# Start of a CIN kernel: transposes in another order, two weights read in memory order, and one block load moved to another queue

## The chip, the cores and the metric

One NeuronCore of one Trainium2 chip. The metric is the device time of one execution in microseconds (us), lower is better. Every execution, the timed ones too, comes with the span and the granted TensorE clock of its core. "Fast" runs are those within 1.5% of the fastest of their kernel; only those are compared. Ratios are the mean time of one kernel's fast runs over that of the kernel before in the same rounds, the first run of each left out, so they are not quite the ratios of the medians quoted beside them.

In the profile PE is TensorE (PEld its weight loads), DVE VectorE, ACT ScalarE, POOL GpSimd and SP SyncE. Where another engine needs the result of an instruction, the program has the instruction raise a semaphore, a counter that the other waits for. Where a wait ends and the profile finds no instruction that had just ended and raises that semaphore, it writes "another core or an unknown queue" in the chain and "remote" in the timeline. There is no other core in this program, so in the lines shown here these words mark semaphores that come late: in the kernel before, TensorE's semaphore records stand at 21.38 and 22.14 us, where the transposes that these waits are for stand as done at 15.64 and 15.87.

## The reference, cut to what matters

Three layers of a compressed interaction network on x (1024 x 39 x 64), then a dense layer to one number per sample:

```python
def _cin_layer(Xk, X0, W, b):          # W: (64, Hk * 39)
    Wr = W.reshape(64, Hk, 39)
    return einsum('bhe,bfe,ohf->boe', Xk, X0, Wr) + b[None, :, None]
for W, b in ((W0, b0), (W1, b1), (W2, b2)):
    Xk = _cin_layer(Xk, X0, W, b)
    outs.append(Xk.sum(axis=-1))
y = concatenate(outs, -1) @ fc_w.T + fc_b
```

Only a sum leaves the last layers, so the kernel folds W2 and fc_w into a small matrix v2, folds v2 and W1 into T, and puts W0 and T side by side as weights over pairs of fields. The main loop multiplies products of gathered rows of x by these weights.

## The kernel before

The parts that the change touches all lie ahead of the main loop; cuts are marked.

```python
# W2 with v: h is inside f, so a step of 39 floats in SBUF
w2v = w2s.rearrange("p (h f) -> p f h", f=F)
for k in range(2):
    for u in range(4):
        f0 = u // 2 * 19 + k * 10
        nc.tensor.matmul(pv[k][32*u : 32*u+32, 0:320], fc2[...], w2v[:, f0 : f0 + 10, :], ...)
# ...
halves = [slice(0, SUB), slice(SUB, BLK)]
for k, cols in enumerate(halves):
    for i in range(3):
        gather_rows(rt[0][:, i, cols], xh[k], i)          # GpSimd, indirect DMA
for k, cols in enumerate(halves):
    gather_rows(rt[0][:, 3, cols], xh[k], 3)
    nc.sync.dma_start(xd[0][0:F, cols], xh[k][0:F])
load(1)                                                   # second block, SP's queue
# ... W1 with v2 into pt, pv; copied to `part` and `rest`; then
for q in range(2):
    for k in (1, 0):                                      # upper rows, lower rows, upper, lower
        rows = slice(H * k, H * k + FT)
        turn_fields(pw[k], part, rows, (q + 1) * NA // 2, q * NA // 2)
turn_fields(pt[0], rest, slice(0, FT), NR)
for k in (1, 0):
    untwine(copies[k], 1, NA * k, NA, NA // 2, pw[k], FT)  # the copies of T into `both`
untwine(copies[1], 1, 2 * NA, NR, 1, pt[0], FT)
spin(3)                                                   # filler matmuls, read by nobody
```

`copies` is VectorE (DVE) for k = 0 and ScalarE (ACT) for k = 1. The pair weights, and so the first main matmul, need all copies of T.

Of the kernel before, what the change touches and what calls it, by code (L numbers as in the profile page):

```python
# [60 lines left out]
B, F, E, H = 1024, 39, 64, 64  # L61
FH = F * H
# [15 lines left out]
NA = 16  # L78
NR = F - 2 * NA
# [19 lines left out]
def cin_kernel(ctx: ExitStack, tc: tile.TileContext, x, w0t, b0, w1, b1, w2, b2, fc_w, fc_b, out):  # L99
    nc = tc.nc  # L100
# [13 lines left out]
    def bank(name):  # L114
        return psum.tile([128, MM], F32, name=name, tag="po")

    def load(n, engine=nc.sync):
        first = n % 2 * FT
        engine.dma_start(  # L119
            xd[n // 2 % NTAB][first : first + F].rearrange("f (b e) -> f b e", e=E),  # L120
            xv[:, n * BB : (n + 1) * BB, :],
        )

    def gather_rows(dst, table, k):
        nc.gpsimd.indirect_dma_start(  # L125
            dst, None, table, bass.IndirectOffsetOnAxis(ap=lists[:, k : k + 1], axis=0)
        )
# [12 lines left out]
    v2 = const.tile([128, H], F32, name="v2")  # L140
# [28 lines left out]
    with prep as prep:  # L169
        w2s = prep.tile([128, FH // 2], F32, name="w2s")  # L170
        w1s = prep.tile([128, FH // 2], F32, name="w1s")
        w0s = prep.tile([128, NW * H], F32, name="w0s")
        part = prep.tile([128, NA, H], F32, name="part")
# [41 lines left out]
        pv = [bank("pv") for _ in range(2)]  # L215
        pt = [bank("pt") for _ in range(2)]
# [5 lines left out]
        def spin(n=1, cols=MM // 2):  # L222
            for _ in range(n):
                nc.tensor.matmul(  # L224
                    idle[:, 0:cols],
                    nc.const_aps.tensor(1.0, (128, 128), F32),
                    nc.const_aps.tensor(1.0, (128, cols), F32),
                    start=True,
                    stop=True,
                )  # L230
# [10 lines left out]
        def new():  # L241
            used[0] += 1
            return tmp[:, used[0] - 1 : used[0]]

        def step(x, at, by, out=None):

            out = new() if out is None else out
            nc.vector.tensor_scalar(out, x, at, by, ALU.is_ge, ALU.mult)
            return out
# [4 lines left out]
        row, f0, j, extra, t, half, q = new(), new(), new(), new(), new(), new(), new()  # L254
# [2 lines left out]
        nc.vector.tensor_copy(row, place)  # L257
        nc.vector.tensor_scalar(parity[:, 1:2], place, 1, None, ALU.bitwise_and)
        nc.vector.tensor_scalar(third, third, 9, None, ALU.logical_shift_right)
        step(row, K, 1.0, extra)  # L260
        nc.vector.tensor_copy(f0, third)
        nc.vector.tensor_scalar(wide[:, 3], shifts[:, 2], row, None, ALU.add)
# [39 lines left out]
        nc.vector.tensor_tensor(field[4], q, step(q, F, -float(F)), ALU.add)  # L302
        nc.vector.tensor_tensor(field[4], field[4], step(q, 56, 11.0), ALU.add)


        nc.vector.memset(w1s[0:H, 0:1], 0.0)
        nc.sync.dma_start(w1s[0:H], w1[:, 0 : FH // 2])

        halves = [slice(0, SUB), slice(SUB, BLK)]
        for k, cols in enumerate(halves):  # L310
            for i in range(3):
                gather_rows(rt[0][:, i, cols], xh[k], i)
        for k, cols in enumerate(halves):
            gather_rows(rt[0][:, 3, cols], xh[k], 3)
            nc.sync.dma_start(xd[0][0:F, cols], xh[k][0:F])
        load(1)



        blocks = prep.tile([128, 2, 320], F32, name="blocks")  # L320
        w2v = w2s.rearrange("p (h f) -> p f h", f=F)
        for k in range(2):
            for u in range(4):
                f0 = u // 2 * 19 + k * 10
                nc.tensor.matmul(
                    pv[k][32 * u : 32 * u + 32, 0:320],
                    fc2[:, u % 2 * 32 : u % 2 * 32 + 32],
                    w2v[:, f0 : f0 + 10, :],
                    start=True,
                    stop=True,  # L330
                )
# [11 lines left out]
                    unit[H * s : H * s + F, H * s : H * s + F],  # L343
                )
        for k in range(2):
            nc.vector.transpose(blocks[:, k], pv[k][:, 0:320])
        column = blocks.rearrange("h k (f j) -> h (k f) j", j=32)[:, :, 0]
        for s, at in enumerate((2, 5)):
            rows = slice(H * s, H * s + H)
            nc.scalar.copy(v2[rows, F:FT], small[rows, at : at + 1])  # L350
        for s in range(2):
            rows = slice(H * s, H * s + H)
# [36 lines left out]
        for s, (a, n) in enumerate(((0, NW), (NW, F - NW))):  # L389
            untwine(copies[s], 0, a, n, 1, pw[s], F)  # L390
        spin()
        w1v = w1s.rearrange("o (h f) -> o f h", f=F)
        for s in range(2):
            rows = slice(H * s, H * s + H)
            nc.tensor.matmul(  # L395
                pv[s][rows, 0 : 32 * NR], v2[rows], w1v[rows, 2 * NA : F, :], start=True, stop=True
            )
        for s in range(2):
            rows = slice(H * s, H * s + H)
            for k in range(2):  # L400
                nc.tensor.matmul(  # L401
                    pt[s][H * k : H * k + H],
                    v2[rows],
                    w1v[rows, NA * k : NA * (k + 1), :].rearrange("o (t j) h -> o j t h", t=2),
                    start=True,
                    stop=True,
                )
        for s, copy in enumerate(copies):
            at = slice(32 * s, 32 * s + 32)
            copy(  # L410
                rest[:, :, at],
                pv[s][H * s : H * s + H, 0 : 32 * NR].rearrange("b (a h) -> b a h", h=32),
            )
        for q in range(2):
            for s, copy in enumerate(copies):
                fields = slice(q * NA // 2, (q + 1) * NA // 2)
                copy(
                    part[:, fields, 32 * s : 32 * s + 32],
                    pt[s].rearrange("b (a h) -> b a h", h=32)[:, fields],
                )  # L420

        def turn_fields(to, src, rows, n, start=0):
            for a in range(start, n, 2):
                m = min(2, n - a)
                nc.tensor.transpose(  # L425
                    to[0 : m * H, a // 2 * FT : a // 2 * FT + FT],
                    src[rows, a : a + m, :].rearrange("b a h -> b (a h)"),
                    unit[rows, rows],
                )

        spin()
        for q in range(2):
            for k in (1, 0):
                rows = slice(H * k, H * k + FT)
                turn_fields(pw[k], part, rows, (q + 1) * NA // 2, q * NA // 2)
        turn_fields(pt[0], rest, slice(0, FT), NR)
# [135 lines left out]
    p = {}  # L572
# [113 lines left out]
```

## Time and profile before

| | before |
|---|---|
| time, median of 4 | 755.05 us |
| main matmuls, busy and idle before them | 723.2 us, 0.0 us |
| first main matmul starts | 24.75 us |
| products of W1 (T) | 11.36 to 14.35 us |
| transposes of T | 14.91 to 15.87 us |
| copies of T begin | 17.86, 21.41, 22.16 us |

TensorE is full from the first main matmul to the last (0.0 us of idle time before the main matmuls), so the only room is the lead, the 25 us ahead of it. Read it as a chain: what the first main matmul waits for, and what that waits for. The lines of it stand in the prediction.

One trap of this profile: the granted clock is shown as 1.00 until the trace's first clock record, which lies at 4.2 us in this trace and between 4.0 and 20.6 us in the others. Whether TensorE was at full or at half clock (1.00 or 0.50 granted) before that is seen only from durations of equal work, such as the four filler records near 4.4 us. In the kernel before (timeline: start, duration, engine, line, operation):

```profile
4.33 0.92 PE L224 MATMUL idle<-const-float32-1.0 128*128 128x256 f32 x4
```

### The profile page before, as it was taken

The numbers are of one execution on the slowest core, as the hardware profiler recorded it, in microseconds if no ns is written. First come the engines' busy times: TensorE is split into PE (matmuls) and PEld (weight loads), VectorE is DVE, ScalarE is ACT, GpSimd is POOL, SyncE is SP. The second block draws the span as 40 slices with busy tenths as digits, with TensorE's granted clock in tenths as the row PEclk, the third lists the DMA queues.
The fourth block names the chain that finished last, engine by engine and source line by source line (L and its number), as shares of the span: only waits on it lengthen the run. The fifth ranks groups of instructions, "written<-read, shape, count | busy, mean of one in ns | idle before, by whom it ended". The sixth has DMA issues, their size and how long they took to land.

```text
span 753.2 us, 5294 instructions
## 1 busy us (share of the span) xinstructions
PE 741.6 (98%) x1913; PEld 324.5 (43%) x1913; DVE 643.1 (85%) x510; ACT 164.1 (22%) x225; POOL 320.5 (43%) x198
## 2 busy tenths in 40 slices
PE   7799999999999999999999999999999999999998
PEld 4344444444444444444444444444444444444443
DVE  4879998888998888889888898888889888898885
ACT  2122122222112212122222212222112221212222
POOL 6568632536333363442536333263532436343100
PEclk9899999999999999999999999999999999999999
DMA  8689977765758766566865758767576854737400
GB/s 213 226 305 367 369 311 252 292 254 174 288 181 328 257 230 269 169 271 245 309 246 192 288 167 317 258 237 261 176 286 224 332 225 162 287 137 307 167 1 0
DMA packets 60223, 180.40 MB, mean 240 GB/s; under 512 B 38415, under 2 KB 38480, under 8 KB 40229
## 3 DMA queue, kind: packets, MB, share of 16 engines
q0 software_dynamic: 24352, 169.12, 59.1%
q1 hardware_dynamic: 34235, 9.27, 5.4%
q10 hardware_dynamic: 1610, 1.67, 1.0%
q8 instruction: 15, 0.25, 0.1%
q14 instruction: 11, 0.09, 0.0%
HBM read 179.98 MB, written 10.60 MB: 253 GB/s over the span
## 4 chain that ended last, share of the span: by engine, by line
PE 97%; DMA 1%; DVE 1%; another core or an unknown queue 0%; POOL 0%; ACT 0%; issue 0%; DVEq 0%; ACTq 0%
PE po L504 96%; DMA w1s<-in_w 1%; PE idle L224 0%; PE pt L401 0%; POOL xh L210 0%; PE tr L488 0%; ACT both L382 0%; PE pv L395 0%; DVE g L543 0%; DVE pairs L453 0%; DVE sums L545 0%; ACT zq L542 0%; PE pw L425 0%; PE small L291 0%
## 5 line engine op out<-in xcount | busy, mean ns | idle before, releaser
L504 PE MATMUL po<-p,wa 128*128 128x512 f32 (+1 forms) x1792 | 723.2, 595 | 0.0
L163 DVE TENSOR_TENSOR p<-r 128x2048 f32<-128x2048 f32 (+2 forms) x196 | 434.8, 2247 | 86.1 <-PE po L504 81.7
L504 PEld LDWEIGHTS po<-p,wa 128*128 128x128 f32 (+1 forms) x1792 | 314.0, 190 | 405.5 <-issue 385.1
L125 POOL DMA_INDIRECT r<-xd,lists x124 | 246.8, 1991 | 355.5 <-DVE p L163 329.5
L523 ACT ACTIVATE z<-po,fc0s 64x512 f32<-64x512 f32 x124 | 84.6, 683 | 354.8 <-PE po L504 348.0
L517 ACT COPY g<-u 39x1024 f32<-39x1024 f32 x64 | 66.6, 1043 | 184.0 <-DVE sums L534 182.4
L529 DVE SCALAR_TENSOR_TENSOR g<-po,b0s,z 64x512 f32<-64x512 f32 x124 | 86.4, 734 | 0.0
L534 DVE TENSOR_REDUCE sums<-g 103x16 f32<-103x1024 f32 x62 | 75.6, 1220 | 2.2
L125 POOL DMA_INDIRECT u<-xd,lists x16 | 36.4, 2277 | 12.5 <-DMA xd<-in_x 8.0
L165 DVE TENSOR_TENSOR p<-u,v 128x2048 f32<-128x2048 f32 x16 | 36.6, 2285 | 0.3 <-PE tr L488 0.3
L125 POOL DMA_INDIRECT v<-xd,lists x16 | 18.0, 1127 | 4.9 <-issue 4.9
L125 POOL DMA_INDIRECT r<-xh,lists x8 | 7.7, 959 | 6.4 <-DVE fields_of L359 4.2
L224 PE MATMUL idle<-const-float32-1.0 128*128 128x256 f32 (+1 forms) x22 | 7.9, 487 | 0.8 <-PEq L673 0.8
L488 PE MATMUL tr<-unit,pairs 128*128 128x128 f32 x7 | 2.2, 318 | 6.3 <-DVE pairs L453 6.3
L382 DVE COPY both<-pw 64x390 f32<-64x390 f32 (+1 forms) x4 | 2.1, 523 | 6.4 <-remote 6.4
L543 DVE SCALAR_TENSOR_TENSOR g<-po,b0s,zq 64x512 f32<-64x512 f32 x4 | 3.0, 742 | 5.3 <-ACT zq L542 5.3
L489 ACT COPY wa<-tr 128x128 f32<-128x128 f32 x7 | 1.9, 266 | 19.9 <-PE tr L488 19.9
L224 PEld LDWEIGHTS idle<-const-float32-1.0 128*128 128x128 f32 x22 | 4.8, 241 | 3.2 <-issue 2.6
L453 DVE TENSOR_TENSOR pairs<-both 128x6 f32<-128x6 f32 (+27 forms) x50 | 5.4, 175 | 0.4 <-ACT both L382 0.4
L542 ACT ACTIVATE zq<-po,fc0s 64x512 f32<-64x512 f32 x4 | 2.7, 684 | 10.2 <-PE po L504 10.2
L488 PEld LDWEIGHTS tr<-unit,pairs 128*128 128x128 f32 x7 | 1.1, 160 | 8.4 <-ACT pairs L457 6.7
L119 POOL DMA_DIRECT2D xd<-in_x x4 | 4.1, 1062 | 0.0
(93 smaller groups left out, 46.4 us busy)
## 6 DMA issues: line engine op xcount, KB each, us to landing
xd<-in_x SPq DMA_DIRECT2D x27, 312.0 KB
r<-xd,lists POOLq DMA_INDIRECT x124
xd<-in_x POOLq DMA_DIRECT2D x4, 312.0 KB
w2s<-in_w ACTq DMA_DIRECT2D x1, 624.0 KB
xh<-in_x ACTq DMA_DIRECT2D x2, 156.0 KB
w1s<-in_w ACTq DMA_DIRECT2D x1, 312.0 KB
w1s<-in_w SPq DMA_DIRECT2D x1, 312.0 KB
xd<-xh SPq DMA_DIRECT2D x2, 156.0 KB
```

What stands on the lines that cost most here:

```text
L119: engine.dma_start(xd[n // 2 % NTAB][first : first + F].rearrange("f (b e) -> f b e", e=E), xv[:, n * BB : (n + 1) * BB, :],)
L125: nc.gpsimd.indirect_dma_start(dst, None, table, bass.IndirectOffsetOnAxis(ap=lists[:, k : k + 1], axis=0))
L163: nc.vector.tensor_tensor(p[:, cols], r[:, i, cols], r[:, k, cols], ALU.mult)
L165: nc.vector.tensor_tensor(p, ut[n // 2 % 2], vt[n // 2 % 2], ALU.mult)
L224: nc.tensor.matmul(idle[:, 0:cols], nc.const_aps.tensor(1.0, (128, 128), F32), nc.const_aps.tensor(1.0, (128, cols), F32), start=True, sto ...
L453: nc.vector.tensor_tensor(out, diagonal(a, b, sa, sb), diagonal(b, a, sb, sa), ALU.add)
L488: nc.tensor.transpose(tr[:, at], pairs[:, c], unit)
L504: nc.tensor.matmul(po[n + h][m], wa[w, c, :], p[w, bass.ts(m, MM)], start=c == opens[n + h], stop=c == closes[n + h],)
L517: nc.scalar.copy(gt[H : H + F], ut[n // 2 % 2][h : h + F, bass.ts(m, SUB)])
L523: nc.scalar.activation(z[m // 2][:, bass.ts(m % 2, MM)], po[n][m][H:128], AF.Identity, bias=fc0s[H:128])
L529: nc.vector.scalar_tensor_tensor(gt[0:H, at], po[n][m][0:H], b0s, z[m // 2][:, at], ALU.add, ALU.mult)
L534: nc.vector.tensor_reduce(sums[:, b_at : b_at + SB], gt.rearrange("p (b e) -> p b e", e=E), AX.X, ALU.add)
```

## The change

Five parts, of two intents: shorten the chain (W1 loaded earlier; W1 and W2 read as they lie in memory, with the reordering left to copies that are made anyway; the transposes that ScalarE waits for issued first), and take the second block's load off SP.

```diff
+        nc.vector.memset(w1s[0:H, 0:1], 0.0)            # was after the field lists
+        nc.sync.dma_start(w1s[0:H], w1[:, 0 : FH // 2])
         ...
             for i in range(3):
                 gather_rows(rt[0][:, i, cols], xh[k], i)
+            if not k:
+                load(1, nc.gpsimd)
         ...
-        load(1)
-        w2v = w2s.rearrange("p (h f) -> p f h", f=F)
+        w2v = w2s.rearrange("p (h f) -> p h f", f=F)
-                    w2v[:, f0 : f0 + 10, :],
+                    w2v[:, :, f0 : f0 + 10],
         ...  (the DVE transposes read PSUM with the step instead)
-        w1v = w1s.rearrange("o (h f) -> o f h", f=F)
+        w1v = w1s.rearrange("o (h f) -> o h f", f=F)
         ...  (the copies to part and rest read PSUM with the step instead)
-        for q in range(2):
-            for k in (1, 0):
+        for k in (1, 0):
+            for q in range(2):
```

More of the change, by code (lines that the diff above doesn't have):

```diff
@@ L303, in cin_kernel @@
         nc.vector.tensor_tensor(field[4], field[4], step(q, 56, 11.0), ALU.add)
-        nc.vector.memset(w1s[0:H, 0:1], 0.0)
-        nc.sync.dma_start(w1s[0:H], w1[:, 0 : FH // 2])
         halves = [slice(0, SUB), slice(SUB, BLK)]
@@ L345, in cin_kernel @@
         for k in range(2):
-            nc.vector.transpose(blocks[:, k], pv[k][:, 0:320])
+            nc.vector.transpose(
+                blocks[:, k].rearrange("p (f h) -> p f h", h=32),
+                pv[k][:, 0:320].rearrange("p (h f) -> p f h", f=10),
+            )
         column = blocks.rearrange("h k (f j) -> h (k f) j", j=32)[:, :, 0]
@@ L395, in cin_kernel @@
             nc.tensor.matmul(
-                pv[s][rows, 0 : 32 * NR], v2[rows], w1v[rows, 2 * NA : F, :], start=True, stop=True
+                pv[s][rows, 0 : 32 * NR], v2[rows], w1v[rows, :, 2 * NA : F], start=True, stop=True
             )
@@ L403, in cin_kernel @@
                     v2[rows],
-                    w1v[rows, NA * k : NA * (k + 1), :].rearrange("o (t j) h -> o j t h", t=2),
+                    w1v[rows, :, NA * k : NA * (k + 1)],
                     start=True,
@@ L411, in cin_kernel @@
                 rest[:, :, at],
-                pv[s][H * s : H * s + H, 0 : 32 * NR].rearrange("b (a h) -> b a h", h=32),
+                pv[s][H * s : H * s + H, 0 : 32 * NR].rearrange("b (h a) -> b a h", h=32),
             )
+        slots = part.rearrange("b (j t) h -> b t j h", t=2)
         for q in range(2):
             for s, copy in enumerate(copies):
-                fields = slice(q * NA // 2, (q + 1) * NA // 2)
-                copy(
-                    part[:, fields, 32 * s : 32 * s + 32],
-                    pt[s].rearrange("b (a h) -> b a h", h=32)[:, fields],
-                )
+                fields = slice(q * NA // 4, (q + 1) * NA // 4)
+                src = pt[s].rearrange("b (h t j) -> b t j h", t=2, h=32)
+                copy(slots[:, :, fields, 32 * s : 32 * s + 32], src[:, :, fields])
         def turn_fields(to, src, rows, n, start=0):
```

## The prediction

> **What bounds the kernel now.** I read the page first (busy times, the chain of waits by line), then the pieces of that chain in order of time, then the timeline and the waits of the first 30 us, then busy time by stage. The page says where the time is:
>
> ```profile
> PE 97%; DMA 1%; DVE 1%; another core or an unknown queue 0%; POOL 0%; ACT 0%; issue 0%; DVEq 0%; ACTq 0%
> ...
> L504 PE MATMUL po<-p,wa 128*128 128x512 f32 (+1 forms) x1792 | 723.2, 595 | 0.0
> ```
>
> The main matmuls occupy 723.2 of 753.2 us with 0.0 us of idle time before them. In the chain they run from 24.96 us to 748.27 us; only small transposes and last-layer products of the same engine stand between. After them come 2.8 us of tail (an activation, a multiply, a sum, the last product). The change touches neither loop nor tail. What it can move is the first 24.96 us, plus the speed of the first few matmuls. That lead is one dependent chain; its pieces:
>
> ```profile
> 5.75 5.47 DMA w1s<-in_w
> 11.22 0.14 issue
> 11.36 0.70 PE pv L395 x2
> 12.05 0.29 PE pt L401
> 12.34 0.12 PE pv L395
> 12.46 1.89 PE pt L401 x5
> 14.35 0.63 PE idle L224 x2
> 14.98 0.66 PE pw L425 x16
> 15.64 0.22 PE pt L425 x4
> 15.87 1.98 PE idle L224 x6
> ...
> 18.30 0.42 ACT both L382
> 18.73 3.41 another core or an unknown queue
> 22.14 0.02 issue
> 22.16 0.28 ACT both L382
> ```
>
> So: the first half of W1 lands at 11.22, the products for T take till 14.35, the transposes of T are issued by 15.87, and only at 22.16 does the last copy of T begin. Between, the timeline of the first 30 us shows the two copying engines waiting although the transposes stand as done:
>
> ```profile
> 14.91 0.73 PE L425 MATMUL pw<-unit,part 40*128 40x40 f32 x16
> 15.48 0.39 PE L425 MATMUL pt<-unit,rest 40*128 40x40 f32 x4
> ...
> 17.86 0.86 ACT L382 COPY both<-pw 64x320 f32<-64x320 f32 x2 [2.83 <-PE idle L224]
> ...
> 21.41 0.99 DVE L382 COPY both<-pw 64x320 f32<-64x320 f32 x2 [6.36 <-remote]
> 22.16 0.55 ACT L382 COPY both<-pt 64x160 f32<-64x160 f32 x2 [3.44 <-remote]
> ```
>
> The three copies wait for TensorE semaphores alone, and these came about 2.2, 5.8 and 6.3 us after the matmul records that should raise them. The profile does not say why. That unexplained stretch of 6.3 us is the largest single piece of the lead, and it decides my uncertainty.
>
> [...] W1 and W2 are read now with h inside f, so with a step of 39 floats (156 bytes): [...] In the main loop a record of 512 columns takes 0.43 us (the chain's 1.72 us for four), so 320 columns would be 0.27. The W2 products are 16 records in four column groups side by side, four rounds, 1.1 us at that rate; the timeline has 2.55 us, over twice that. [...] Here matmul outputs stay contiguous, but the changed copies and transposes now read PSUM with steps of 7, 10 or 16 floats. No run here shows what that costs a copy. [...] DMA share 0.90 from 5.75 to 11.36 us[...]. [...] The stage table shows a granted clock of 0.50 from 22.16 to 24.96, after TensorE stood idle.
>
> **The change, part by part.**
> W1 load: its memset moves from 5.66 us to behind the fourth small DVE instruction, so SP can issue at about 1.5 instead of 5.75. W1's first half then lands long before 11.22. The 312 KB move in front of W2 and W0; at the 390 KB per us that the queue reached in its best early slice that is up to 0.8 us of delay. I put W2's arrival at 6.5 us instead of 5.8.
> W2 in memory order: [...] 1.3 us instead of 2.55, so done at 7.8 against 8.47. The two DVE transposes (0.52 each) and copies into v2 follow as before: v2 complete near 9.1 against 9.8. But the W0 transposes and one filler matmul stand ahead on TensorE, and they ended at 10.06 and 10.68; W0 itself comes a little later. So W1's products start at about 10.6 rather than 11.36: 0.7 gained of the 1.5 that the landing at 11.22 seems to cost.
> W1 in memory order: per array quarter at most one 224-column product (two records of 0.19) and one 512-column product (two of 0.43), [...] 1.5 against 2.99. Gain 1.5 us.
> Copies with a step: the part copies are two in a row on each engine, 0.76 us together on DVE. If a PSUM step costs a third, 0.25 is given back; the DVE transposes may give back 0.1 off the path.
> Sum up to the transposes of T: 0.7 + 1.5 - 0.25, about 2 us earlier.
> Transposes of T: the same 20, upper rows first. ACT's tile is complete after 8 instead of 12. At 0.04 us apiece in the record that is nothing by itself. The last copy (the remaining fields) still follows all 20, so the path's end depends on whether the delayed semaphores remain.
> Second block: SP's load, issued at 12.33, becomes one GpSimd issue (1.06 us each by the page's existing four) between third and fourth gather. It delays five gathers by about 1.3 us. In exchange the u gather, which waited 7.96 us till 28.27 for that load, starts some 4 us earlier. Nothing on the path reads u before 41.80, so this is worth nothing at the end, except less traffic of small packets in the critical stretch.
>
> **The rivals.**
> A, the delay stays relative to the transposes (same 20 instructions, same fillers): the gain is the 2 us, with half clock still. 753.1 us. For it: no instruction is taken away.
> B, the delay is set by something at an absolute time or by the total of what TensorE issued before (a backlog that drains): coming earlier only lengthens the wait. 754.5 to 755.1. For it: the last filler's semaphore came right behind the last transpose's, although 1.5 us of fillers lay between, so completions, not array work, were late.
> C, the delay comes from alternating between upper and lower rows, or from the loads competing then. Both are changed, so it vanishes: T would be copied by about 15.5 us and the first main matmul could be near 17. Then the gathers bind: they are 512 KB each, eight of them at about 415 GB/s (stage table) take 10 us, the second-half ones land after 22 us, and the GpSimd issue makes them later. So of 8 us some 5 to 7 remain, with the half clock gone or shorter: 748 to 750. Against it: the W0 transposes alternate only once and show no delay, but traffic differed too.
> D, a loss: W2 delayed more than assumed, stepped PSUM reads at double cost, gathers later. Each is under 1 us against a gain of 2; 755.5 at worst.
>
> **Range and chances.** A 0.4, B 0.3, C 0.25, D 0.05. The weighted mean is near 752.6; I take 752.8 us, with 747.5 to 755.5 holding A, B and most of C. Faster by 2% means under 740.0; that needs 15 us of a lead of 25, which the gathers and W2's own arrival forbid: 0.01. Slower by 2% would need the main loop to change: 0.01. Within 2%: 0.98.
>
> **What would show it right or wrong.** Right: the main matmuls again 723 us with no idle time; W2's products near 1.3 us and W1's near 1.5 in the timeline; the W1 landing gone from the chain of waits; part copies 0.4 to 0.55 us; first main matmul near 23 us. A is told from B and C by the time from the last transpose's record to the last copy of T: 6.3 us again (A), longer (B), or below 1 us (C, where DVE's first products should then wait for gathers). Wrong: strided reads not the cause of the slow products (they stay above 2 us), W0 or W2 arriving over 1 us later, or late gathers of the second block leaving the main loop with gaps after 36 us.

## The result, and the profile after

749.49 us (749.30 to 749.92, 4 runs) against 755.05 us, ratio 0.9928 with a 95% interval of 0.9911 to 0.9945. That is 5.6 us, inside the range and 3.3 us below the point.

The main loop is what it was (page, groups by line: busy time and mean, then idle time):

```profile
L507 PE MATMUL po<-p,wa 128*128 128x512 f32 (+1 forms) x1792 | 722.5, 595 | 0.0
```

The spans in the two traces differ by 5.5 us: 4.8 us of it is the lead, the other 0.7 us the main matmuls themselves, of which fewer ran at half clock in the new trace: from 19.95 us until the clock record at 21.80, against 24.75 until 28.05 in the kernel before. The chain of waits of the changed kernel, in order of time:

```profile
9.91 0.63 PE idle L224 x2
10.54 0.34 PE pv L398 x2
...
11.08 1.41 PE pt L404 x6
...
12.52 0.34 ACT rest L413
12.86 1.10 another core or an unknown queue
...
13.99 0.38 ACT part L423
...
14.50 1.35 PE pw L428 x16
15.85 0.39 PE pt L428 x4
16.24 2.86 PE idle L224 x6
19.09 0.21 PE tr L491
19.31 0.85 PE idle L224 x2
20.16 1.71 PE po L507 x2
```

The W1 landing is gone from it. The unexplained wait of 3.41 us behind the transposes is gone too: the copies of T begin at 15.39, 15.89 and 16.28. A smaller one, 1.10 us in the chain, has appeared earlier: the copies of W1's products into `part` start at 13.93 and 13.99, though the last of those matmuls stands as done at 11.95. The first main matmul starts at 19.95 instead of 24.75. It could have been earlier: at half clock the six filler matmuls from 16.17 on took 2.93 us instead of 1.57, and the first transpose of the pair weights, whose input was done at 17.73, came behind them at 18.89. Here the filler itself is on the chain.

The W2 products hardly became faster, 2.31 us against 2.55 (timelines of the changed kernel):

```profile
4.44 1.65 PE L224 MATMUL idle<-const-float32-1.0 128*128 128x256 f32 x4
6.02 2.31 PE L325 MATMUL pv<-w2s,fc 128*32 128x320 f32 x16
```

The fillers tell why: 1.65 us where the kernel before has 0.92, so TensorE was still at half clock (six fillers took 2.93 us in this trace where the granted clock was 0.50, and 1.57 in the kernel before at 1.00). The trace's first clock record, to full, is at 8.1 us here.

### The profile page after: what moved, and what is told of

Its sections match the earlier page's. It is cut to its first block, busy times and chain, and to the rows that moved or that the text cites. A ratio compares the mean times of both kernels' runs of the same rounds, so it can differ in the third digit from the quotient of the medians.

```text
span 747.7 us, 5294 instructions
## 1 busy us (share of the span) xinstructions
PE 741.8 (99%) x1913; PEld 326.2 (44%) x1913; DVE 643.1 (86%) x510; ACT 164.4 (22%) x225; POOL 326.8 (44%) x199
## 4 chain that ended last, share of the span: by engine, by line
PE 99%; DVE 0%; POOL 0%; ACT 0%; another core or an unknown queue 0%; issue 0%
PE po L507 97%; PE idle L224 1%; PE pv L325 0%; PE pt L404 0%; PE pw L428 0%; POOL xh L210 0%; PE pw L340 0%; PE tr L491 0%; DVE g L546 0%; DVE sums L548 0%; ACT zq L545 0%; PE small L294 0%; PE small L292 0%; PE pt L428 0%
## 5 line engine op out<-in xcount | busy, mean ns | idle before, releaser
L507 PE MATMUL po<-p,wa 128*128 128x512 f32 (+1 forms) x1792 | 722.5, 595 | 0.0
L125 POOL DMA_INDIRECT r<-xd,lists x124 | 251.3, 2027 | 352.2 <-DVE p L163 330.9
L125 POOL DMA_INDIRECT v<-xd,lists x16 | 16.6, 1037 | 4.9 <-issue 4.9
L224 PE MATMUL idle<-const-float32-1.0 128*128 128x256 f32 (+1 forms) x22 | 9.9, 598 | 0.8 <-PEq L676 0.8
L548 DVE TENSOR_REDUCE sums<-g 103x8 f32<-103x512 f32 x4 | 2.7, 686 | 0.1
```

The costliest lines, as they stand in the source:

```text
L125: nc.gpsimd.indirect_dma_start(dst, None, table, bass.IndirectOffsetOnAxis(ap=lists[:, k : k + 1], axis=0))
L224: nc.tensor.matmul(idle[:, 0:cols], nc.const_aps.tensor(1.0, (128, 128), F32), nc.const_aps.tensor(1.0, (128, cols), F32), start=True, sto ...
L507: nc.tensor.matmul(po[n + h][m], wa[w, c, :], p[w, bass.ts(m, MM)], start=c == opens[n + h], stop=c == closes[n + h],)
```

## The experiments

Twelve runs of nine kernels, in four batches. A batch runs on one chip, and the chip mattered (the kernel before took about 755 us in batches 1 and 3, 750.02 and 750.59 in 2 and 4): batches 1 and 3 were on the same chip, batches 2 and 4 on two others. Three theories of the late semaphores were named ahead: T1, they follow any dense burst of TensorE instructions; T2, the alternation between upper and lower rows causes them; T3, the second block's load by SP does.

### Batch 1: one part of the change undone at a time

`u_order`, the old order of the transposes:

```diff
-        for k in (1, 0):
-            for q in range(2):
+        for q in range(2):
+            for k in (1, 0):
```

> The changed kernel with the old order of the transposes of T (upper and lower rows alternating by quarter). Changed kernel: ratio 0.9928, 749.5 us. Theory T1 (TensorE's semaphores come late after any dense burst of its instructions, wherever it lies, and each part of the change shortens the path by itself): 749.5 to 750.3, copies of T within 1 us of their transposes. T2 (the alternation of row halves causes the late semaphores): the 6.3 us wait after the transposes is back, 754 to 756. T3 (the second block's small packets, sent by SP, cause it): no change, 749.5.

Measured: 748.88 us (747.82 to 750.30), before 754.96; ratio 0.9905, interval 0.9865 to 0.9946. The intervals of this batch are wide because two of the eleven runs of the kernel before fell out, at 873.99 (slow state) and at 763.94 us (counted as fast). The medians serve better. The copies of T began at 15.38, 15.44 and 16.26 us in the alternating order; their transposes were over at 14.07. So some 1.3 us of lateness, not 6. T2 falls.

`u_w1`, W1 read with the step again, with the old copies:

```diff
-        w1v = w1s.rearrange("o (h f) -> o h f", f=F)
+        w1v = w1s.rearrange("o (h f) -> o f h", f=F)
         ...  (matmul operands and copies as before)
```

> The changed kernel with W1 read across memory again (step of 39 floats) and the old copies out of PSUM. T1: W1's products take 3 us instead of 1.5, but the burst is thinner and their semaphores come on time, so the net loss is 0 to 1.5 us: 749.5 to 751. If the products' time simply adds: 751. T2 and T3: 751, no other change.

Measured: 748.66 us (747.46 to 750.97), ratio 0.9910 (0.9868 to 0.9951): nothing lost that these runs can show. That is below the 751 us that T2 and T3 expected, although W1's products took 3.10 us (9.95 to 13.05) as foreseen. The chain of this trace says why: it does not run through T but through gathers of the first block, the last of which landed at 23.3 us; those of `u_order` (26.5 us) and `after_again` (25.1 us) do the same. The clock was full early in this trace (four fillers in 0.92 us), which makes it a clean measurement of the W2 read (timeline):

```profile
4.26 0.92 PE L224 MATMUL idle<-const-float32-1.0 128*128 128x256 f32 x4
5.36 1.37 PE L325 MATMUL pv<-w2s,fc 128*32 128x320 f32 x16 [0.18 <-DMA w2s<-in_w]
```

W2 in memory order at full clock takes 1.37 us, the kernel before took 2.55 with the step at full clock. So the step did roughly halve the rate.

`u_load`, W1's first half loaded at the old place:

```diff
-        (after the fourth small instruction)  nc.sync.dma_start(w1s[0:H], ...)
+        (after the field lists)               nc.sync.dma_start(w1s[0:H], ...)
```

> The changed kernel with the first half of W1 loaded at the old place (SP issue near 5.75 us). All theories: W1 lands near 11.2 us, so W1's products start 0.7 us later; T1 adds that the pause thins the burst, so part is won back: 749.5 to 750.2.

Measured: 750.05 us (748.30 to 753.52), ratio 0.9932 (0.9890 to 0.9974). The chain goes through that landing again and W1's products start at 11.14, as expected; on the whole time it is within the scatter.

`u_gps`, the second block loaded by SP again:

```diff
-            if not k:
-                load(1, nc.gpsimd)
+        load(1)        # SP, after the copies of the first block
```

> The changed kernel with the second block loaded by SP again after the copies of the first (and not by GpSimd behind three gathers). T1 and T2: within 0.5 us of the changed kernel (749.5), later u gather without effect. T3: the late semaphores after the transposes are back, 753 to 755.

Measured: 755.37 us (751.98 to 756.49), ratio 0.9983 (0.9940 to 1.0025). This one line takes back the whole gain. The wait is there again (VectorE idles 7.09 us before its copy of T, 6.36 in the kernel before; chain of waits):

```profile
14.88 0.76 DVE part L422 x2
15.63 7.07 another core or an unknown queue
22.73 0.48 DVE both L384
```

T1, which expected no change here, falls as the reason for the 5.6 us; T3 stands.

### Batch 2: on another chip

`after_again` is the changed kernel unaltered.

> The changed kernel unaltered, for comparison on this chip: 749.5 us (748.5 to 750.5), ratio 0.9925 to 0.993; copies of T within 1 us of their transposes.

Measured: 749.55 us (748.56 to 751.22), as expected. But the kernel before, which had taken 755 until now, took 750.02 on this chip (748.52 to 751.75, 11 runs, all fast). The ratio is 0.9994, interval 0.9976 to 1.0012. **On this chip the change gains nothing that can be told from zero.**

`a_gps` is the kernel before with that one part alone:

```diff
+            if not k:
+                load(1, nc.gpsimd)
         ...
-        load(1)
```

> The kernel before with one part of the change: the second block loaded by GpSimd behind three gathers. T3 (SP's load of the second block makes TensorE's semaphores late): the 6.3 us wait after the transposes shrinks to under 1.5 us, first main matmul at 19 to 21 us instead of 24.75, 749 to 751 us, most of the whole gain. T1 and T2: 754.5 to 755.5.

Measured: 748.17 us (747.72 to 749.15), ratio 0.9975 (0.9959 to 0.9991). It is better than the kernel before, by 1.9 us in the medians, and better than the whole change by 1.4 us; the two intervals just overlap. The chain has the main matmuls start at 19.82 us, as T3 expected, but with no trace of the kernel before on this chip that shows no wait removed.

`sp_big` moves the same bytes through SP in large packets. The result is wrong on purpose, because the block then lies in another order:

```diff
-                load(1, nc.gpsimd)
+        nc.sync.dma_start(xd[0][FT : FT + F],
+            x[BB : 2 * BB].rearrange("b f e -> (b f e)").rearrange("(r c) -> r c", c=BLK))
```

> Wrong result on purpose. The changed kernel with the second block loaded by SP at the old place, same 312 KB, but copied as it lies in memory: some dozens of large packets instead of 1,248 of 256 bytes. If the number of small packets makes the semaphores late (T3a): no late semaphores, 748.5 to 750.5. If it is SP's queue or the load's time or bytes as such (T3b): as with the small packets, 754 to 756.

Measured: 750.30 us, ratio 1.0006 (0.9989 to 1.0024), wrong as intended. On a chip where the kernel before shows no loss this tells nothing apart.

`sp_late` loads by SP in small packets, but only after the copies of T:

```diff
-                load(1, nc.gpsimd)
+        nc.sync.dma_start(gate, both[H : H + 1, 2 * NA * FT : 2 * NA * FT + 1])  # waits for T
+        load(1)
+        (the gathers of that block and what follows on GpSimd come after it)
```

> The changed kernel with the second block loaded by SP, small packets again, but held back until the copies of T are done (a tiny transfer that waits for the last copy stands before it in SP's queue). T3 with coincidence in time as the cause: no late semaphores after the transposes of T, first main matmul near 20 us; the second block lands after 25 us, the u gather after that, so the main loop may have a gap near 37 us of up to 2 us: 749.5 to 752. If SP's load harms wherever it stands: 754 or more.

Measured: 750.35 us (749.04 to 752.99), ratio 1.0001 (0.9982 to 1.0019). The timeline shows the lead with no late semaphore anywhere, and so what binds next:

```profile
12.70 1.03 PE L421 MATMUL pw<-unit,part 40*128 40x40 f32 x16
13.48 0.86 ACT L378 COPY both<-pw 64x320 f32<-64x320 f32 x2 [0.64 <-PE pw L421]
...
17.93 1.29 DVE L165 TENSOR_TENSOR p<-r 128x512 f32<-128x512 f32 x2 [2.19 <-DMA r<-xh,lists]
18.77 2.05 PE L510 MATMUL po<-p,wa 128*128 128x512 f32 x2 [2.15 <-DVE p L165]
```

T's copies are under way at 13.48, before the last transposes are issued, and yet the first product waits for its gather until 17.9. The first weights were ready at 16.49, and TensorE stood idle for 2.15 us. So behind the late semaphores stand the gathers, here some 2 us further on than the weights. Later TensorE has a gap of 2.3 us in this trace, from 45.46 to 47.80, while VectorE makes a product; in `sp_late_2` the chain waits there for a gather that landed at 45.34. A gap of up to 2 us was expected near 37 us.

### Batch 3: back on the first batch's chip

`before_again` is the kernel before, unaltered, for its trace.

> The kernel before, unaltered, to have its trace beside the others on the same chip. On a chip where it takes 755 us: the copies of T wait till about 22 us and the main matmuls start near 25 us, as in its first trace. On a chip where it takes 750 us (as in the second batch): copies of T within 2 us of their transposes, main matmuls from 19 to 20.5 us; then the 5 us of the change are the late semaphores alone, and they are a property of the chip as much as of the kernel.

Measured: 754.73 us, ratio 1.0007 (0.9991 to 1.0022). The lateness sits elsewhere this time, but ends at the same point. The chain of waits:

```profile
12.08 1.89 PE pt L401 x5
13.97 0.63 PE idle L224 x2
14.60 3.80 issue
18.40 1.10 PE pw L425 x16
19.50 1.38 PE pt L425 x4
```

ScalarE got the semaphore of W1's products at 17.97 (they stand as done at 13.97), so the transposes came late, and the last copy of T began at 21.78 against 22.16 in the first trace; the first main matmul started at 23.94. What varies is which semaphore is late; what is common to the two traces is that the last copy of T comes at about 22 us.

`a_gps_2` repeats `a_gps` here.

> The kernel before with the second block loaded by GpSimd behind three gathers and nothing else, again. Where the kernel before takes 755: 748.5 to 750.5 (T3), the whole gain or slightly more; where it takes 750: about 748.2 as in the second batch.

Measured: 749.18 us (748.57 to 750.96), before 754.47; ratio 0.9924, interval 0.9911 to 0.9938. One part of five gives 5.3 us on the chip where the kernel before takes 755. The whole change gave 0.9928 in its own measurement (not of the same rounds). The long wait behind the transposes is gone (timeline), though TensorE idled another 1.02 us, unexplained, ahead of the first main matmul at 20.79:

```profile
15.79 0.39 PE L426 MATMUL pt<-unit,rest 40*128 40x40 f32 x4
16.02 0.86 ACT L383 COPY both<-pw 64x320 f32<-64x320 f32 x2 [0.57 <-PE pw L426]
...
17.53 0.55 ACT L383 COPY both<-pt 64x160 f32<-64x160 f32 x2 [0.65 <-PE pt L426]
```

`sp_big_2` repeats `sp_big` here.

> Wrong result on purpose. The changed kernel with SP loading the second block at the old place in large packets, again. Where the kernel before takes 755: 749 to 751 if the small packets are the cause (T3a), 754 to 756 if it is SP's load as such (T3b). Where the kernel before takes 750 it tells nothing apart: 750.

Measured: 762.85 us (761.20 to 763.84), ratio 1.0113 (1.0098 to 1.0129). With 37,170 packets under 512 bytes (counted in `sp_big`, the same program) instead of 38,415 in the kernel before, over the whole run, so without those of the second block, it is 8 us worse than the kernel before. Chain of waits:

```profile
18.20 0.42 ACT both L387
18.62 6.91 another core or an unknown queue
...
26.13 0.21 ACT pairs L462
26.34 4.28 another core or an unknown queue
30.62 0.25 ACT wa L494
...
30.91 2.08 PE po L509 x2
```

So the number of small packets is not the cause; it was my favourite. T3b, which expected 754 to 756, has the direction right and misses the size. What this kernel has more of is gathers, and that they are to blame is only argued: GpSimd issued the u gather, which needs the second block, at 20.64 us without a wait for it, where the kernel before waited 7.96 us for the block until 28.27, and went on with one gather every 1.24 us. The lateness lasted until 30.6.

### Batch 4: a third chip

`sp_late_2` was to tell whether SP's load beside the gathers is what harms, or whether the pause that the load makes in GpSimd's gathers (1.08 us of issue in the changed kernel) is what helps.

> The changed kernel with SP loading the second block (small packets) only after the copies of T, again, for a chip where the kernel before takes 755 us. There: if the semaphores are late because SP's load runs beside the gathers in that stretch (T3c), the copies of T start within 1.5 us of their transposes, first main matmul 18.5 to 21 us, whole time 749 to 753.5 (a gap of about 2 us near 45 us from the late u gather, as in the second batch). If the pause that the load makes in GpSimd's gathers is what helps (T3d), the pause is missing here and the copies of T wait till about 22 us or later, 754 to 758. Where the kernel before takes 750 us: 750.3 as before, and nothing told apart.

Measured: 751.20 us (749.08 to 753.52), ratio 1.0007 (0.9973 to 1.0040), the kernel before 750.59 (747.76 to 755.13). This chip, too, shows no loss in the kernel before, so the question was not reached, and it stays open.

### What the traces say together

I compared, for each trace, the instructions of the three engines that raise a semaphore in the first 28 us with the semaphore records, and counted those with no record within 0.2 us of their end. On the chip of batches 1 and 3 these are 9 to 29 per trace, and 11 and 23 in the first traces of the two kernels. On the other two chips they are 1 or 2 in each of the five traces. After 28 us they are 0 to 4 in any trace. So semaphores are late on the chip where semaphore records are also missing (up to 28 us the first traces have 74 records for 81 raises in the kernel before, 70 for 93 in the changed kernel, on the three engines' own semaphores). Within that chip the count does not go with the loss: it is highest, 29, in `a_gps_2`, which is fast, and 11 in the kernel before.

That may point at the recording itself, which no run here tests. Since every run was recorded, no run shows what the kernel does unrecorded. Whether the 5 us exist there is not settled.

## Why the prediction was right or wrong

The time was in the range; the point was 3.3 us too high. That it fell inside is in part the width of the range, which held A, B and most of C; the path that was worked out, 2 us less up to the transposes and the wait unchanged, is not what happened. By its steps:

- **Where the time can come from.** Right: 722.5 us of main matmuls without idle time, 4.8 us of the gain in the lead and 0.7 us in the speed of the first main matmuls.
- **W1 load and the start of its products.** Right in the first trace: predicted 10.6, measured 10.47 us. But where the clock stayed at half (`after_again`: the two fillers from 11.27 us took 1.22, 0.70 in the first trace) the W0 transposes ahead of them took 2.23 us instead of 1.19, and the products started at 12.43.
- **W1 in memory order, 1.5 us instead of 2.99, an estimate of mine.** Right at full clock: 10.47 to 11.95. At half clock (`after_again`) 12.43 to 15.14, 2.7 us.
- **W2 in memory order, 1.3 us, an estimate of mine.** The step was the cause (2.55 us with it), and the size was right only at full clock: 1.37 (`u_w1`). Why the step costs this much was not shown. In the changed kernel's own trace it took 2.31. W2 itself did not come later, as feared (6.5 us): its products began at 6.02. The step that failed was the silent assumption of a full clock at 6 us; I read it off a page that shows 1.00 there.
- **A third more for the copies out of PSUM.** Wrong: 0.76 us on DVE and 0.65 us on ACT for two part copies, before and after. The term was 0 instead of 0.25 us.
- **"Sum up to the transposes of T, about 2 us earlier."** Right up to W1's products, which ended 2.40 us earlier (11.95 for 14.35). Wrong at the transposes: they began 0.4 us earlier (14.50 for 14.91) and ended later (16.23 for 15.87), because the copies between came 2 us after the products and the clock fell to half (record at 14.97 us). So the 4.8 us of the lead do not come from this sum. They come from the stretch behind it: from the last transpose's record to the last copy of T 0.05 us instead of 6.29.
- **The second block's load "worth nothing at the end, except less traffic of small packets".** This was the failed step. It is the part that carries the gain: undone, 755.37 us; alone, 749.18. And the exception I gave it, fewer small packets, is wrong too, as `sp_big_2` shows. How the load delays the semaphores, by running beside the gathers or by not pausing them, stays open. The u gather did start earlier, at 21.85 instead of 28.27, by 6.4 us and not 4.
- **The rivals.** A, the most likely in the prediction (the delay stays relative to the transposes), did not occur. C, with a chance of 0.25, came nearest: it named alternation or the competing loads, the bind by the gathers (not in the first trace's chain, but in those of `u_order`, `u_w1`, `after_again` and `sp_late`), and 748 to 750 us. Of its two causes alternation is refuted (`u_order`) and the second block's load confirmed. Its detail was wrong: half clock stayed (0.53 from 15.87 to 22.16 us in the stage table), and part of the lateness moved to W1's products. B's picture, a backlog that drains to a fixed time, fits the kernel before in its two traces (22.16 and 21.78) but not the changed kernel.
- **What was not foreseen at all.** The gain depends on the chip: 5.6 us where the kernel before takes 755, nothing that can be told from zero where it takes 750.

Why the whole change was not better than its one part on the second chip I can only argue. In the four traces that read W2 with the step, the first record of full clock is at 4.2 to 10.1 us. In the ten that read it in memory order it is at 4.0 to 8.5 us in five and at 16 us or later in five. That the shorter products are why it rises later is my guess, which was not shown. At half clock the faster read gains little: 2.31 to 2.36 us (2.31 in the changed kernel) against 2.57 with the step (`before_again`, `a_gps`). A rival is chance: in these traces the clock changes only at whole multiples of 3.41 us from one change to the next (17.07, 6.83 and 727.04 us in the first trace of the kernel before, 6.83, 6.83 and 727.04 in that of the changed kernel), so the first full record would also depend on where the start fell in that step. The records can set this aside in part. Counted within a step of 3.41 us, seven traces have their changes at 2.4 to 3.3 us: of these the three that read W2 with the step (`before_again`, `a_gps`, `a_gps_2`) rise at 9.3 to 10.1 us and the four in memory order (`after_again`, `u_gps`, `sp_big`, `sp_late_2`) at 16.0 to 16.6. But those four also load W1 early, and no run isolates the read.

The smallest edit with the whole gain is the kernel before with the one line of `a_gps` (`u_w1` and `u_order`, at 748.66 and 748.88, lie within its scatter, in other rounds): 749.18 us where the kernel before takes 754.47, and 748.17 where it takes 750.02.

## What to carry to other kernels

When a chain waits on a semaphore long after the instruction that raises it stands as done (6.3 us here), treat that gap as its own term: find by undoing one part at a time which neighbour it depends on, and repeat the kernel before on several chips before believing in the gain. What a change that shortens TensorE's work saves in a start-up stage has to be told at the clock that is granted there (W2 in memory order saved 1.2 us at full clock here and about 0.2 at half); read the clock from equal work, not from the page alone (which showed 1.00 where the fillers took 1.65 us). And look for the next bound before adding more: here the gathers stood close behind the weights (about 2 us in `sp_late`).
